# Two interleaved streams of graph batches: the distance between the streams set to 136 units in place of 111

## The chip, the core and the metric

The kernel runs on one core of one Trainium2 chip. The metric is the device time of one execution in microseconds. Five engines work side by side, each from its own queue and in the order of that queue: TensorE (PE; its weight loads are listed apart as PEld), VectorE (DVE), ScalarE (ACT), GpSimd (POOL) and SyncE (SP, which here only issues DMAs).

## What is computed

Sixteen graphs ("batches") of N = 1024 nodes with 256 features pass through four attention layers with a residual each. The batches don't depend on each other. Cut to what matters:

```python
x: (16, 1024, 256) f32        adj: (16, 1024, 1024) int32, 0 or 1, same for all layers
for layer in 0..3:
    h  = relu(layernorm(x))
    Wh = h @ W                               # layer 3: four heads of 64 columns each
    e  = act(Wh @ a1 [rows] + Wh @ a2 [columns])        # N x N scores
    p  = softmax of e (layer 1: exp(-e)) over the edges only
    y  = p @ Wh
    x  = x + y            # layers 1 and 2: x + elu(y)
    # layer 3: x + layernorm_per_head(relu(y + bias) + Wh)
```

## The kernel before, in words

All that follows is in `short_path`. (A second path, `general_path`, is entered at the end only when the inputs fall outside a tested range; here it isn't.)

**One batch.** `batch(b)` (L364) is a Python generator that issues the instructions of one batch, and ends each portion with a `yield` of a number, its nominal duration in units of about 1 us. Its portions are:

- *Projection of layer 0*, four pairs of 128-node tiles (L475 to L484). `project` (L278) has three steps of 0.5, 1.0 and 2.5 units: centre and square (L285 on DVE, L292 on ACT, and the inverse root on POOL, L271 and L272), transpose on PE (L301) and copy to `hT` on ACT (L303), then matmul (L308) into an accumulator in PSUM and evict it into `V` (L376, L380). Four pairs make 16 units.
- *Three times `attend`* (L408), for layers 0, 1 and 2. It first needs the `row` tile in PSUM. `weigh` (L317) fills it by PE (L337) and then makes eight 128x1024 weight tiles from it on DVE (L330), each of which feeds two accumulations on PE (L424, eight yields of 0.9). Then the other six 128-node outputs follow (3.6 units each), each is finished on ACT and DVE (L348 to L360, or L464), and after each second one the projection of the next layer is worked in (4 units). In sum 49.4 units.
- *Layer 3* (L493 to L654), 52.2 units. For each of four heads, `weigh3` makes eight weight tiles (L330 again; `row` by L337 or L529), PE accumulates values and totals in 32-column tiles (L541), ACT copies the sums (L618), PE turns them back (L625, L633), DVE scales them into `y` (L636), and `center` (L498) adds the bias on POOL (L502), adds the projected features `h3` on DVE (L503) and takes mean and variance (L505 to L511). `rescale` (L514) follows one head later. The output leaves by DMA (L650).

So a batch is 16 + 3 x 49.4 + 52.2 = 216.4 units, without waits.

**The two streams.** `stream(0)` issues batches 0, 2, 4, ..., 14 one after another, `stream(1)` batches 1, 3, ..., 15. Each stream has a clock that its yields advance, and a loop takes the next portion from the stream whose clock is behind:

```python
streams = [[0.0, stream(0)], [LAG, stream(1)]]
while streams:
    ahead = min(streams, key=lambda s: s[0])
    t = next(ahead[1], None)
    ...
        ahead[0] += t
```

`LAG` (L74) is where the clock of stream 1 starts. Before its first batch, each stream spends 8 units on issuing its loads (`load`, L119). The order of issue is what the framework fills the engines' queues from. It may bring an instruction forward that is ready earlier, except where `tc.keep_in_program_order` holds it.

**What the streams share.** One `row` tile (`bufs=1`, L324): a list, `row_taken`, lets only one stream use it, and the other yields 0.25 units (L322), or the rest of the `start` loop (L339), until it is given back. One `h3` and one `y` (pool `single`, `bufs=1`, L391 and L494). `h3` is written first by `evict3` (L397) in the first projection for layer 3, inside `attend(2, ...)`, and read last by L503 of head 3, at the end of layer 3. Two accumulators in PSUM for each stream (L276), two `misc` tiles in PSUM, three masks and three node tiles `x_b`, and eight weight tiles for each stream.

Of the kernel before, what the change touches and what calls it, by code (L numbers as in the profile page):

```python
# [61 lines left out]
def short_path(ctx: ExitStack, tc: tile.TileContext, ins: dict, out: bass.AP, bad: bass.AP):  # L62
# [8 lines left out]
    NH = N // HALF  # L71
    NG = HALF // P
    EXT = [3, 3, 3, 3 * H]
    LAG = 111.0  # L74
    QUAD = P // 4
    ROOT_D = D**0.5
    ROOT_E = E**0.5
# [579 lines left out]
    def stream(first: int):  # L657
        for _ in loading[first]:
            yield 2.0
        for b in range(first, B, 2):  # L660
            yield from batch(b)
# [3 lines left out]
    next(preparing)  # L665
    streams = [[0.0, stream(0)], [LAG, stream(1)]]
    while streams:
# [311 lines left out]
def tile_gat4(  # L979
# [27 lines left out]
    nc.vector.memset(ones, 1.0)  # L1007
    n_bad = flags.tile([1, 1], I32, name="n_bad")
    short_path(tc, ins, out, bad)
    with tc.tile_pool(name="flag_psum", bufs=1, space=bass.MemoryType.PSUM) as psum:  # L1010
        bads = psum.tile([1, 1], F32, name="bads")
# [39 lines left out]
```

## Time and profile before

| | |
|---|---|
| three runs | 2948.02, 2948.88, 2951.19 us (median 2948.88) |
| the profiled execution | 2950.02 us, of which the span of the trace is 2948.4 us |
| PE busy | 2810.6 us, 95% of the span |
| DVE busy | 2124.8 us, 72% |
| ACT busy | 1092.1 us, 37% |
| POOL busy | 980.7 us, 33% |
| granted TensorE clock, mean | 0.992 |

The page divides the span into 40 slices, and PE is at nine tenths or more in all of them but the first and the last two. So the questions to put to this profile are asked of short windows: where PE is idle, how often that place comes back, and what the other engines do there. A table of windows gives for each stretch the busy time of every engine with the number of instructions in brackets, and after that the granted clock, the share of the DMA engines and what they moved.

### The profile page before, as it was taken

The page shows a single profiled execution, that of the slowest core. Times are in us where ns is not written, and L with a number is a line of the kernel's source. Part 1 is how long each engine was busy: PE and PEld are TensorE (multiplying, and loading weights), DVE is VectorE, ACT ScalarE, POOL GpSimd, SP SyncE. Part 2 cuts the span into 40 slices and gives each one's busy share as a digit, 9 for nine tenths or more (in the row PEclk, how much of TensorE's full clock was granted, in tenths as well). Part 3 has the DMA queues.
Part 4 walks back from the last instruction along what each step waited for, and adds up shares of the span by engine and source line. Part 5 has one row for each costly group of instructions (what it writes and reads, how often), then busy time and mean ns, then how long its engine had stood idle before and what let it go on. Part 6 is the DMA issues. An engine that isn't in the chain of part 4 may idle for free.

```text
span 2948.4 us, 44754 instructions
## 1 busy us (share of the span) xinstructions
PE 2810.6 (95%) x16790; PEld 1969.3 (67%) x16790; DVE 2124.8 (72%) x4471; ACT 1092.1 (37%) x3025; POOL 980.7 (33%) x1535
## 2 busy tenths in 40 slices
PE   7999999999999999999999999999999999999975
PEld 5775857668576685766758576685766857667551
DVE  5658688585976858678586875859768586785855
ACT  2333434343343433424333343433434334343331
POOL 2123324243233423324233242432334233242333
PEclk9999999999999999999999999999999999999997
DMA  7204022030311303122030220303113031010101
GB/s 123 40 8 65 29 31 56 8 51 29 42 45 19 68 1 51 36 29 58 8 52 29 33 55 8 51 29 45 43 20 67 1 51 36 15 30 8 22 18 27
DMA packets 120495, 106.11 MB, mean 36 GB/s; under 512 B 73680, under 2 KB 91216, under 8 KB 120272
## 3 DMA queue, kind: packets, MB, share of 16 engines
q0 software_dynamic: 40448, 67.12, 15.4%
q1 hardware_dynamic: 79824, 36.05, 5.5%
q8 instruction: 135, 2.21, 0.3%
q14 instruction: 88, 0.72, 0.1%
HBM read 153.49 MB, written 33.55 MB: 63 GB/s over the span
## 4 chain that ended last, share of the span: by engine, by line
PE 60%; DVE 23%; issue 8%; POOL 5%; ACT 3%; DMA 1%; POOLq 0%; SPq 0%; ACTq 0%; DVEq 0%
PE acc L424 36%; DVE weights L330 16%; PE acc L541 11%; PE acc L308 9%; PE misc L301 2%; POOL rstd L272 2%; POOL y L502 2%; ACT square L292 1%; DVE V L380 1%; PE row L337 1%; DVE y L503 1%; DVE var L511 1%; DVE y L507 1%; DVE mean L505 1%; ACT below L356 1%
## 5 line engine op out<-in xcount | busy, mean ns | idle before, releaser
L424 PE MATMUL acc<-V,weights 128*128 128x257 f32 x6144 | 1436.3, 385 | 33.9 <-DVE weights L330 16.7
L424 PEld LDWEIGHTS acc<-V,weights 128*128 128x128 f32 x6144 | 1141.9, 191 | 277.9 <-DVE weights L330 72.0
L541 PE MATMUL acc<-weights,V 128*32 128x512 f32 x6144 | 692.0, 597 | 12.1 <-DVE weights L330 8.1
L330 DVE SCALAR_TENSOR_TENSOR weights<-row,ex,mask 128x1024 f32<-128x1024 f32 x512 | 629.1, 1273 | 97.4 <-PE row L529 66.0
L308 PE MATMUL acc<-W,hT 128*128 128x259 f32 (+1 forms) x2048 | 516.5, 389 | 41.7 <-ACT hT L303 29.2
L330 DVE SCALAR_TENSOR_TENSOR weights<-row,V,mask 128x1024 f32<-128x1024 f32 x384 | 473.8, 1275 | 1.0 <-PE row L337 1.0
L308 PEld LDWEIGHTS acc<-W,hT 128*128 128x128 f32 x2048 | 379.6, 191 | 138.0 <-ACT hT L303 47.1
L541 PEld LDWEIGHTS acc<-weights,V 128*32 128x32 f32 x6144 | 189.6, 110 | 417.6 <-issue 410.7
L356 ACT ACTIVATE below<-acc,inv 128x256 f32<-128x256 f32 x256 | 121.1, 473 | 818.0 <-DVE inv L349 537.3
L272 POOL TENSOR_TENSOR rstd<-rstd,minus_half 128x2 f32<-128x2 f32 (+1 forms) x320 | 302.9, 947 | 20.3
L292 ACT ACTIVATE square<-x_b,minus_mean 128x256 bf16<-128x256 f32 x512 | 259.7, 507 | 111.1 <-DVE minus_mean L282 105.4
L404 POOL TENSOR_TENSOR x_b<-x_b,beta 128x256 f32<-128x256 f32 x128 | 93.4, 730 | 489.8 <-ACT square L292 489.8
L348 DVE TENSOR_SCALAR inv<-acc 128x1 f32<-128x1 f32 x256 | 39.2, 154 | 256.0 <-PE acc L424 254.7
L271 POOL TENSOR_SCALAR rstd<-squared 128x2 f32<-128x2 f32 x256 | 64.6, 253 | 462.8 <-ACT square L292 461.9
L303 ACT ACTIVATE hT<-misc 128x512 f32<-128x512 f32 x256 | 150.1, 592 | 119.7 <-PE misc L301 119.4
L359 DVE SCALAR_TENSOR_TENSOR x_b<-below,x_b 128x256 f32<-128x256 f32 x256 | 133.0, 519 | 85.3 <-ACT below L356 83.2
L618 ACT COPY sums<-acc 128x512 f32<-128x512 f32 x128 | 74.9, 585 | 307.8 <-PE acc L541 300.3
L285 DVE TENSOR_SCALAR centered<-x_b,minus_mean 128x256 f32<-128x256 f32 x512 | 182.6, 385 | 5.3
L376 ACT ACTIVATE V<-acc,rstd 128x3 f32<-128x3 f32 x384 | 98.4, 261 | 232.0 <-PE acc L308 231.3
L380 DVE TENSOR_SCALAR V<-acc,rstd,V 128x256 f32<-128x256 f32 x256 | 131.6, 537 | 62.0 <-ACT V L376 61.1
L301 PE MATMUL misc<-ident,centered 128*128 128x128 f32 x1024 | 157.9, 277 | 15.2 <-DVE centered L285 13.4
L149 POOL DMA_DIRECT2D adj_i<-in_adj_dram x128 | 74.7, 584 | 286.4 <-ACT adj_i L154 254.9
(88 smaller groups left out, 2210.0 us busy)
## 6 DMA issues: line engine op xcount, KB each, us to landing
adj_i<-in_adj_dram POOLq DMA_DIRECT2D x128, 256.0 KB, 3.9
x_b<-in_x_dram SPq DMA_DIRECT2D x16, 1024.0 KB, 6.4
narrow<-in_adj_dram POOLq DMA_DIRECT2D x64, 256.0 KB, 9.5
out_dram<-y POOLq DMA_DIRECT2D x32, 512.0 KB, 7.4
mask<-narrow SPq DMA_TRANSPOSE x64, 3.7
W<-in_L_gnn_W_dram SPq DMA_DIRECT2D x3, 256.0 KB, 5.8
weights<-in_L_gnn_a_dram SPq DMA_DIRECT2D x3, 256.0 KB, 8.1
W<-in_L_gnn_W_dram SPq DMA_DIRECT2D x2, 128.0 KB, 8.3
```

Source lines behind the costliest of these rows:

```text
L272: nc.gpsimd.tensor_tensor(r, r, minus_half.to_broadcast([P, n]), op=ALU.pow)
L285: nc.vector.tensor_scalar(centered[:, n, :], xb[:, 2 * pair + n, :], minus_mean[:, n : n + 1], 0.0, op0=ALU.add, op1=ALU.max,)
L292: nc.scalar.activation(square, xb[:, 2 * pair + n, :], AF.Square, bias=minus_mean[:, n : n + 1], accum_out=squared[:, n : n + 1],)
L301: nc.tensor.transpose(turned[:, k, ts(n, P)], centered[:, n, ts(k, P)], ident)
L303: nc.scalar.mul(hT, turned, ROOT_D)
L308: nc.tensor.matmul(projected, hT[:, k, ts(n, P)], W[l][:, k, :], start=(k == 0), stop=(k == NK - 1),)
L330: nc.vector.scalar_tensor_tensor(w, r, c(j), masks[b][:, j // 2, :, j % 2], op0=op, op1=ALU.mult)
L356: nc.scalar.activation(below, acc[:, :D], AF.Exp, scale=inv)
L359: nc.vector.scalar_tensor_tensor(xi, below, 1.0, xi, op0=ALU.min, op1=ALU.add)
L380: nc.vector.tensor_scalar(V[:, i, :D], projected[:, :D], rstd, V[:, i, D : D + 1], op0=ALU.mult, op1=ALU.mult,)
L424: nc.tensor.matmul(accs[i], weights[j][:, ts(i, P)], V[:, j, : D + 1], start=(j == 0), stop=(j == NI - 1),)
L541: made = nc.tensor.matmul(accT[ts(n, QUAD), :], values, moving, start=first, stop=last)
```

## The change

One constant, the start of the second stream's clock, goes from 111 to 136 units:

```diff
@@ -71,7 +71,7 @@
     NH = N // HALF
     NG = HALF // P
     EXT = [3, 3, 3, 3 * H]
-    LAG = 111.0
+    LAG = 136.0
     QUAD = P // 4
     ROOT_D = D**0.5
     ROOT_E = E**0.5
```

No instruction is added or taken away. The order changes in which the portions of the two streams are issued. Of a batch of 216.4 units, 136 are 0.628, about five eighths, and 111 are 0.513.

## The prediction

> **What bounds the kernel now.** I read the page's table of engines first.
>
> ```profile
> PE 2810.6 (95%) x16790; PEld 1969.3 (67%) x16790; DVE 2124.8 (72%) x4471; ACT 1092.1 (37%) x3025; POOL 980.7 (33%) x1535
> ```
>
> PE is the bound, and is idle for 2948.4 - 2810.6 = 137.8 us. The change adds and removes no instruction, so it can only move those 137.8 us. Next, the period: SyncE's timeline shows one fetch of `x_b` at each end of a batch.
>
> ```profile
> 1023.51 0.38 SPq L115 DMA_DIRECT2D x_b<-in_x_dram  x1
> 1202.24 0.37 SPq L115 DMA_DIRECT2D x_b<-in_x_dram  x1
> ```
>
> A batch ends, in one stream or the other, every 178.73 us. Then the windows of one period:
>
> ```profile
> 1024.00:1094.00 70.00, 69.83 (x339) 59.87 (x338) 39.78 (x112) 24.39 (x75) 20.03 (x42) 1.00 0.10 31
> 1094.00:1164.00 70.00, 68.54 (x506) 35.63 (x505) 65.07 (x99) 21.97 (x52) 17.99 (x29) 1.00 0.33 39
> 1164.00:1184.00 20.00, 20.00 (x123) 14.06 (x123) 13.51 (x31) 9.79 (x23) 11.24 (x10) 1.00 0.32 54
> 1184.00:1204.00 20.00, 17.43 (x93) 14.29 (x93) 15.10 (x39) 12.12 (x40) 12.99 (x19) 1.00 0.21 28
> ```
>
> The reader should see two gaps in PE (second column). From 1094 to 1164 one stream is in layer 3, DVE is 93% busy and PE loses 1.46 us. From 1184 to 1204 a batch ends and the next one starts: PE loses 2.57 us. With 0.17 before, a period loses 4.2 us. Last the end, where stream 1 is alone:
>
> ```profile
> 2800.00:2820.00 20.00, 14.54 (x53) 10.49 (x52) 15.52 (x24) 4.06 (x12) 8.19 (x9) 0.83 0.14 52
> 2820.00:2850.00 30.00, 28.63 (x138) 23.79 (x136) 11.74 (x44) 13.56 (x42) 11.69 (x23) 1.00 0.00 1
> 2850.00:2860.00 10.00, 3.72 (x19) 2.17 (x22) 6.13 (x6) 2.24 (x8) 5.25 (x15) 0.92 0.00 0
> ```
>
> Alone, the weighing stage of an `attend` loses 5.46 us of PE, its rest 1.37 us in 30, and the step into layer 3 another 6.28 us.
>
> **What the Trainium skill says.** "Perfetto Trace Analysis", Identifying the Most-Contended Engine, warns that matmul busy time doesn't tell how near PE is to its peak. Agreed here: PE is 95% busy and its weight loads 67%; so I use idle time alone and leave PE's rate as it is. The same page, Optimization Strategy, says that a gap which comes back on the bounding engine can mean that there is no room for the next tile. The 2.57 us of before aren't that (DVE and ACT chains fill it), but the step below with `h3` would be. "TensorE: Matmul & The Clock Gate", What's actually happening, says that an idle PE falls to a lower clock until it has been busy again. The trace agrees: the granted clock is 0.83 over 2800 to 2820 and 1.00 in every steady window above. A long gap so costs more than its length.
>
> **The change, part by part.** I place everything by the nominal clock in the code. Within a batch: projection of layer 0 at 0 to 16; the three `attend` from 16, 65.4 and 114.8, the first 7.2 units of each being the weighing; layer 3 from 164.2 to 216.4.
>
> *Before*, a stream in layer 3 waits some 6 units for `row`, which the other stream's layer 1 takes between heads; a batch therefore lasts 222.3 units, and 111 is just half of it. The streams end alternately every 111.15 units, so a unit is 178.73 / 111.15 = 1.608 us. Batch start (0 to 16) lies against 111 to 127 of the other stream, the weighing of layer 2: eight L330 of 1.275 us (10.2 us of DVE) meet the projection's own DVE work and the end of layer 3. That is the 2.57 us gap.
>
> *After*, working through the yields, no stream finds `row` taken, so a batch lasts 216.4 units, and the gaps between starts alternate: 136 from an even batch to the odd one, 80.4 from the odd to the next even one.
>
> (1) *Starts of even batches, and of batch 1* (8 of the 15 starts with a partner). They now lie against 80 to 98 of the partner (batch 1: against 136), the middle of an `attend`, where PE has eight matmul groups ready and DVE no weighing. I put the remaining gap at 0.8 us, between 0.17 (the quiet 70 us above) and the 2.57 of today. Gain 8 x (2.57 - 0.8) = 14.2 us.
>
> (2) *Starts of odd batches from batch 3* (7). They lie against 136 of the partner, after the weighing of layer 2. That collision goes too, but another arrives: `h3` has one buffer. The even batch writes it first at 114.8 + 7.2 + 3.6 + 0.5 + 3.6 + 1.0 + 3.6 = 134.3 (L397). The odd batch reads it last in `center` of head 3, at 214.4 of its own, when the partner stands at 214.4 - 80.4 = 134.0. Before, the same reading stood at 220.4 - 111.2 = 109.2, so 25.1 units ahead of the write. The trace has that distance in us (lines L503 and L397 of the same pair of batches):
>
> ```profile
> L503 DVE SCALAR_TENSOR_TENSOR y<-y,h x1: 691/691/691, 1013.4 to 1013.4; 128x512 f32<-128x512 f32 x1
> L397 ACT ACTIVATE h<-acc,rstd x1: 466/466/466, 1048.8 to 1048.8; 128x256 f32<-128x256 f32 x1
> ```
>
> From the end of L503 (1014.1) to L397 are 34.7 us of room. The change takes away 25.1 - 0.3 = 24.8 units, 39.9 us. So L397 comes 5.2 us too early and has to wait. Behind it on ACT are the partner's projections; on PE, the projected tiles hold both accumulators of that stream, so its L424 stop. PE has only the new batch's projection to fill in. That is the unknown cost. Lower bound: the 10.5 us of PE work in that projection (by the page's busy times of L308 and L301 over 16 batches of 4 layers: (516.5 + 157.9) / 64) cover it and the gap falls to 0.8 as in (1). Upper bound: the whole chain from the last L541 (ending near 1003.3) to the end of L503, 10.7 us, is lost. I take the wait itself, uncovered, and the 0.8: 6.0 us, because the new batch's projection needs ACT, which is the engine that waits. Cost 7 x (6.0 - 2.57) = 24.0 us.
>
> (3) *Layer 3 against the rest* (15 times). Before, 40 L330 fall in 37 units. After, in layer 3 of an odd batch, 40 in 38 (the partner's layer 2 starts right after head 3's weighing); of an even batch, 32 in 31 and eight more at its quiet end. About as dense; I leave the 1.46 us each at that: nothing. DVE's saturation was covered by matmuls of the partner, and still is. Bounds: all 15 gaps gone, -22 us, or see the third rival.
>
> (4) *The start alone.* Stream 0 runs 25 units more by itself, through the weighing of layer 2: 5.46 us from the end's own window. Its partner before was the batch start counted in (1).
>
> (5) *The end alone.* When batch 14 is done, batch 15 stands at 80.4 instead of 111.2; 30.8 units more of quiet `attend` run alone, some 26 us at 1.37 in 30: 1.2 us. The last weighing, layer 3 and the tail are alone as before.
>
> (6) *DMAs.* SP's fetch of `x_b` is released by the end of another batch and then has 80 units, 129 us, to its use; it took 6.4 us to land. Masks likewise. Nothing, and 129 us of cover. POOL's queue carries the same instructions; in (2) its share of projection and `center` meet, which is in the upper bound.
>
> Sum: -14.2 + 24.0 + 0 + 5.5 + 1.2 = +16.5 us on the profiled 2950.0, so 2966.5; that execution was 1.1 us above the median of the runs, so I say 2965.
>
> **Rivals.** *Other side: the wait is covered.* If the planner places the new batch's projection, or more of the partner's products, under the 5.2 us, all fifteen starts fall to 0.8: -15 x 1.77 + 6.7 = -19.9, 2929 us. It decides below 3.6 us for each odd start, where 7 x (3.6 - 2.57) equals the 7.5 us that the rest of the sum gains. For it: those 10.5 us of independent work. Against: ACT is 60% busy there already and waits in order. *Nothing to measure:* the odd starts cost about what they cost now, and the ends eat the gain: 2949 - 7.5 + 7 x 1 = 2948. *Layer 3 becomes DVE-bound:* the wait for `row` used to give layer 3 six more units; without it, DVE has some 78 us of work in the odd batch's dense 38 units (40 L330, 51 us; `center` and scaling of three heads, seven operations of 0.7 us each, 14; the partner's finishing and projecting, 4.8 us in each 11.2 units of `attend`, for 31 units, 13), and 38 units last 38 x 1.608 = 61 us. Before it was 71 us (51, 14 and 6) in 37 units, 59 us. If 5 us of that reach PE in seven places, on top of my sum: 2965 + 35 = 3000 us. Against: 12 us of excess cost only 1.46 today. That the change does nothing is excluded, since the order of issue differs by 25 units throughout.
>
> **How the numbers follow.** Forecast (waits of 4 to 10 us, 2955 to 2990) 0.47; covered (2920 to 2943) 0.24; nothing to measure 0.16; DVE-bound 0.13. About 0.2% (5.9 us) is what a measurement of this kernel can tell from no change. Faster 0.24, same 0.16, slower 0.47 + 0.13 = 0.60. The range, 2930 to 2990, leaves out half of the covered case and most of the DVE-bound one, 0.2. The forecast's own range is 2955 to 2990.
>
> **What would show it.** Right: PE idle at every second batch end some 6 us, at the others under 1; the first L397 directly behind L503 of the other batch; an idle of PE or ACT ended by DVE L503; ends of batches apart by 80 and 136 units in turn, some 130 and 220 us; no more waits of layer 3 for `row`. Wrong: both kinds of ends alike, L397 tens of us after L503, or more than 2 us of idle PE in the DVE-bound stretches.

## The result and the profile after

The median is 3023.66 us of five runs (3022.9 to 3028.71), against 2949.01 before: ratio 1.0254, 95% interval 1.024 to 1.0268. That is 74.7 us slower, where 16 were forecast, and above the range. The page's first lines of the changed kernel:

```profile
span 3021.4 us, 44651 instructions
PE 2827.2 (94%) x16790; PEld 1967.5 (65%) x16790; DVE 2169.3 (72%) x4471; ACT 1095.7 (36%) x3025; POOL 974.9 (32%) x1535
```

The instructions are the same. The span is 73.0 us longer: PE is idle for 194.2 us in place of 137.8 (+56.4) and busy 16.6 us longer, at a mean granted clock of 0.984 in place of 0.992.

SyncE's timeline tells the ends of batches, by the fetch of `x_b`:

```profile
887.87 0.37 SPq L115 DMA_DIRECT2D x_b<-in_x_dram  x1
1023.60 0.38 SPq L115 DMA_DIRECT2D x_b<-in_x_dram  x1
1254.10 0.37 SPq L115 DMA_DIRECT2D x_b<-in_x_dram  x1
```

Ends follow each other after 135.7 and 230.5 us in turn, in the order that the nominal clock gave and both some 5% longer (129 and 219). A pair of batches lasts 366.2 us, where two of before last 357.5. From the first output (292.6, before 308.8) to that of batch 14 (2856.7, before 2812.45) the seven pairs cost 60.5 us more than before, and the stretches alone at both ends the other 12.5.

One pair in windows. An even batch is in the middle of layer 3 in the second line and ends in the third, at 1023.6; an odd one is in the middle of layer 3 in the fifth and ends in the sixth.

```profile
887.87:960.00 72.13, 71.83 (x457) 48.82 (x456) 56.60 (x105) 23.60 (x63) 21.70 (x42) 1.00 0.30 52
960.00:1000.00 40.00, 37.21 (x283) 18.68 (x281) 27.98 (x52) 10.22 (x25) 13.76 (x16) 1.00 0.31 54
1000.00:1030.00 30.00, 25.39 (x119) 20.17 (x120) 27.17 (x64) 16.06 (x49) 18.52 (x25) 1.00 0.30 67
1030.00:1180.00 150.00, 149.20 (x808) 116.39 (x810) 95.04 (x222) 54.24 (x158) 30.86 (x63) 1.00 0.12 16
1180.00:1215.00 35.00, 31.02 (x236) 16.03 (x240) 31.78 (x47) 13.79 (x32) 13.44 (x15) 0.95 0.31 50
1215.00:1254.10 39.10, 36.34 (x211) 25.97 (x204) 31.84 (x67) 18.64 (x52) 23.27 (x31) 0.96 0.18 24
```

First minus second number of a line is PE's idle time. Against two periods of before:

| PE idle in a pair of batches, us | before | after | forecast |
|---|---|---|---|
| layer 3, both batches | 1.46 + 1.46 | 2.79 + 3.98 | as before |
| end of the even batch | 2.57 | 4.61 | 0.8 |
| end of the odd batch | 2.57 | 2.76 | 6.0 |

So the loss went to layer 3 and to the even end, and not to the odd end, where I had put it. Of the 8.7 us that the pair is longer, 6.8 are idle PE and 1.9 are PE work that took longer.

The list of waits names the waiting instruction, then what it waited for, the total in us, the times and the longest. PE now waits for VectorE. After:

```profile
PE misc L301 <- DVE centered L285: 47.5, 26, 13.9
PE row L337 <- DVE weights L330: 18.8, 7, 2.7
```

Before, the first of these waits came to 13.4 us, and the second was not in the list:

```profile
PE misc L301 <- DVE centered L285: 13.4, 3, 12.8
```

(The longest in each, 12.8 and 13.9 us, is PE's wait for its first work at the very start.) And VectorE in turn waits for GpSimd, and ScalarE for VectorE. After:

```profile
DVE y L503 <- POOL y L502: 90.1, 49, 4.0
ACT h L397 <- DVE y L503: 7.3, 7, 1.1
```

Before, there was no such wait of L397, and of the other this much:

```profile
DVE y L503 <- POOL y L502: 27.4, 33, 2.9
```

`center` takes `y` from VectorE (L636) to GpSimd for the bias (L502) and back to VectorE (L503). The longest case after, from the timelines of VectorE and GpSimd (start and duration in us; in brackets how long the engine was idle and for whom):

```profile
963.96 0.69 DVE L636 TENSOR_TENSOR y<-misc,inv 128x512 f32<-128x512 f32 x1
964.08 0.72 POOL L272 TENSOR_TENSOR rstd<-rstd,minus_half 128x2 f32<-128x2 f32 x1
964.78 1.27 POOL L516 TENSOR_TENSOR y<-y,gamma 128x512 f32<-128x512 f32 x1
966.13 1.27 POOL L517 TENSOR_TENSOR y<-y,x_b 128x512 f32<-128x512 f32 x1
967.36 1.27 POOL L502 TENSOR_TENSOR y<-y,bias 128x512 f32<-128x512 f32 x1
968.66 0.69 DVE L503 SCALAR_TENSOR_TENSOR y<-y,h 128x512 f32<-128x512 f32 x1 [4.01 <-POOL y L502]
```

GpSimd works off three operations (L272, L516, L517) before the bias, and VectorE stands still in the middle of layer 3, with L503 at the head of its queue. The same hop, of the second head, before the change:

```profile
1155.93 0.68 DVE L636 TENSOR_TENSOR y<-misc,inv 128x512 f32<-128x512 f32 x1
...
1156.60 1.28 DVE L330 SCALAR_TENSOR_TENSOR weights<-row,ex,mask 128x1024 f32<-128x1024 f32 x1
1158.01 0.69 DVE L503 SCALAR_TENSOR_TENSOR y<-y,h 128x512 f32<-128x512 f32 x1
```

Here the queue has one L330 of 1.28 us between the two (and, where the dots stand, an L282 of 0.16 us), and it covers the hop. Not every hop before was covered by an L330. In the four heads of a batch VectorE idled 0.2, 0.1, 0 and 1.2 us in front of L503: an L330 stood between in the first two, small operations of the next projection in the other two. After the change it idles 1.4, 4.0, 1.4 and 0 us in an even batch and 2.4, 2.1, 0.2 and 0 us in an odd one, and in the five longest of these nothing at all stands between. Over the eight heads of a pair that is 11.5 us after and 3.0 before: 8.5 us more, for a pair that is 8.7 us longer. That near equality is only a hint, and the experiments have to show that the one causes the other.

How the hop reaches PE can be followed at one place, the second head of the odd batch:

```profile
1197.94 0.69 DVE L503 SCALAR_TENSOR_TENSOR y<-y,h 128x512 f32<-128x512 f32 x1 [2.13 <-POOL y L502]
1204.12 6.04 DVE L330 SCALAR_TENSOR_TENSOR weights<-row,ex,mask 128x1024 f32<-128x1024 f32 x5
1210.21 1.97 PE L337 MATMUL row<-ident,V 128*128 128x128 f32 x8 [2.68 <-DVE weights L330]
```

VectorE's queue, 2.13 us late, works off the L330 that still read `row`, and PE can fill the one `row` anew only after the last of them.

### The profile page after: what moved, and what is told of

Its sections match the earlier page's. It is cut to its first block, busy times and chain, and to the rows that moved or that the text cites. A ratio compares the mean times of both kernels' runs of the same rounds, so it can differ in the third digit from the quotient of the medians.

```text
span 3021.4 us, 44651 instructions
## 1 busy us (share of the span) xinstructions
PE 2827.2 (94%) x16790; PEld 1967.5 (65%) x16790; DVE 2169.3 (72%) x4471; ACT 1095.7 (36%) x3025; POOL 974.9 (32%) x1535
## 5 line engine op out<-in xcount | busy, mean ns | idle before, releaser
L330 DVE SCALAR_TENSOR_TENSOR weights<-row,ex,mask 128x1024 f32<-128x1024 f32 x512 | 629.9, 1275 | 47.0 <-PE row L529 42.6
L308 PE MATMUL acc<-W,hT 128*128 128x259 f32 (+1 forms) x2048 | 527.7, 395 | 46.3 <-ACT above L358 21.2
L308 PEld LDWEIGHTS acc<-W,hT 128*128 128x128 f32 x2048 | 372.5, 191 | 168.6 <-ACT above L358 43.4
L330 DVE SCALAR_TENSOR_TENSOR weights<-row,V,mask 128x1024 f32<-128x1024 f32 x384 | 471.3, 1273 | 15.2 <-PE row L337 15.2
L272 POOL TENSOR_TENSOR rstd<-rstd,minus_half 128x2 f32<-128x2 f32 (+1 forms) x320 | 300.6, 940 | 19.6
L285 DVE TENSOR_SCALAR centered<-x_b,minus_mean 128x256 f32<-128x256 f32 x512 | 197.9, 423 | 4.7
L301 PEld LDWEIGHTS misc<-ident,centered 128*128 128x128 f32 x1024 | 122.1, 142 | 104.1 <-issue 50.3
L154 ACT ACTIVATE adj_i<-adj_i,minus_half 128x1024 bf16<-128x1024 bf16 x128 | 147.3, 1151 | 14.1 <-DMA adj_i<-in_adj_dram 14.1
L509 ACT ACTIVATE wide<-y 128x512 f32<-128x512 f32 x64 | 40.3, 630 | 308.1 <-DVE y L507 291.0
```

What stands on the lines that cost most here:

```text
L154: square = nc.scalar.activation(adj_i, adj_i, AF.Square, bias=minus_half, accum_out=squares[:, b, i : i + 1])
L272: nc.gpsimd.tensor_tensor(r, r, minus_half.to_broadcast([P, n]), op=ALU.pow)
L285: nc.vector.tensor_scalar(centered[:, n, :], xb[:, 2 * pair + n, :], minus_mean[:, n : n + 1], 0.0, op0=ALU.add, op1=ALU.max,)
L301: nc.tensor.transpose(turned[:, k, ts(n, P)], centered[:, n, ts(k, P)], ident)
L308: nc.tensor.matmul(projected, hT[:, k, ts(n, P)], W[l][:, k, :], start=(k == 0), stop=(k == NK - 1),)
L330: nc.vector.scalar_tensor_tensor(w, r, c(j), masks[b][:, j // 2, :, j % 2], op0=op, op1=ALU.mult)
```

## The experiments

My theory at the start was that the loss sits at particular meeting places of 136 (`h3`, and the hand-over of `row` near 1210 us, where PE waits 2.68 us). The rival was that any unequal spacing does harm because VectorE gets too full. Times below are medians, ratios are to the kernel before in the same job.

**Other distances.** The edit is the constant alone:

```diff
-    LAG = 136.0
+    LAG = 130.0   # x1;  124.0 in x2;  142.0 in x3
```

> LAG 130: batches start 130 and 86.4 units apart in turn, still without any wait for row in the nominal clock, but layer 2 of the even batch now asks for row 6 units after head 3 of the odd batch has given it back, and first writes h3 some 10 us later than at 136. Theory 'these places' (the cost sits in the row hand-over at 1210 us and in the meeting at h3, both special to 136): at least 3 us a pair of batches back, 2995 to 3005 us. Theory 'spacing' (any spacing but the half leaves layer 3 beside the partner's finishing stages with VectorE too full): 3005 to 3025 us.

Measured: 3064.81 us, ratio 1.0384 (1.0367 to 1.0402).

> LAG 124: starts 124 and 98.4 units apart, and both batches of a pair wait for row in layer 3 again, so a batch lasts 222.4 units as at 111. Theory 'spacing': between 111 and 136, about 2975 to 3000 us. Theory 'the wait for row is what spaced layer 3 out' (the slide of 6 units is what was lost): within 10 us of before. Theory 'these places': within 15 us of before, too.

Measured: 3045.99 us, ratio 1.0321 (1.0304 to 1.0338).

> LAG 142: starts 147.8 and 74.7 units apart, even batches wait for row, odd ones' first write of h3 comes even earlier against the partner's last read (5.7 units before it). Theory 'h3': the stall of ScalarE grows by some 9 us a pair, over 3060 us. Theory 'spacing': 3030 to 3050 us. Theory 'these places' without h3: below 3023 us.

Measured: 3061.63 us, ratio 1.0379 (1.0362 to 1.0396).

All three are slower than 136. So nothing special to 136 is the cause: my theory of the places falls, and so does the one that the wait for `row` had protected layer 3, as 124 has that wait by its nominal clock and still loses 95 us. What remains is the spacing, though it costs more than its expectation said at every point. The 142 case met the number of the theory on `h3`, and shows how little such a match proves: in its trace ScalarE waits for L503 seven times, 14.8 us in all, 2.1 us each and not 9.

**Two buffers for `h3`.**

```diff
-            h3 = last["h3"] = single.tile([P, NI, D], F32, name="h3")
+            h3 = last["h3"] = single.tile([P, NI, D], BF, name="h3", bufs=2)
```

> LAG 136 with two h3 in bfloat16 in the room of one in float32 (h3 is rounded to bfloat16, the rest of the computation is kept). The forecast's step on h3: 7 stalls of 5.2 us gone, 2985 to 2990 us. What the trace of 136 shows instead (L397 directly behind L503, ScalarE idle for 1.05 us there): 3010 to 3023 us.

Measured: 3013.25 us, ratio 1.0215 (1.0198 to 1.0232). `h3` accounts for 10 of the 75 us, 1.5 us a pair of batches, and in this trace L397 no longer waits for L503. The meeting that I had worked out exists, but ScalarE loses 1.05 us at it and not 5.2.

**Less work on VectorE in layer 3.**

```diff
             if h == H:
                 return iter(())
+            if h % 2 == 1:
+                weights.extend(weights[-NI:])
+                return iter(())
```

> LAG 111, with heads 1 and 3 of layer 3 taking over the weight tiles of heads 0 and 2 (their own 256 L330 and 256 of the small row matmuls are left out, so their output is that of other weights): VectorE has 326 us less to do. PE-bound as the kernel before is, it can only win back idle PE in layer 3, at most 1.46 us x 15: 2920 to 2950 us.

Measured: 2952.76 us, ratio 1.0008 (1.0002 to 1.0015).

> The same at LAG 136 (heads 1 and 3 take over the weights of heads 0 and 2). Theory 'VectorE is too full in layer 3 beside the partner's finishing': the distance of 75 us to LAG 111 shrinks to under 30 us. Theory 'shared port of GpSimd and VectorE, or the places of h3 and row': it stays at 50 us or more.

Measured: 2972.91 us, ratio 1.0079 (1.0062 to 1.0096). At 111, some 300 us less work on VectorE (1819.4 us busy in place of 2124.8) gain nothing: there it isn't the bound. At 136 they gain 51 us, and the distance between the two shrinks from 75 to 20 us. So at 136 the time passes through VectorE's queue in layer 3. Whether through its work or its waits, this doesn't tell. (The port of the second expectation is taken up in the last section.)

**Less work on GpSimd in layer 3.** The bias addition and the multiplication by gamma are left out.

```diff
-            nc.gpsimd.tensor_add(yh, yh, bias[:, head].unsqueeze(1).to_broadcast(shape))
...
-            nc.gpsimd.tensor_mul(yh, yh, gamma[:, head].unsqueeze(1).to_broadcast(shape))
```

> LAG 111 without the bias addition and the multiplication by gamma in layer 3 (L502 and L516 left out, 166 us of GpSimd): both lie off PE's path except at the batch ends, where the chain through them is 2.6 us shorter: 2925 to 2950 us.

Measured: 2936.03 us, ratio 0.9953 (0.9936 to 0.997).

> The same at LAG 136 (bias addition and gamma left out). Theory 'small VectorE operations are held up while GpSimd works' (VectorE is 44 us busier after the change without one instruction more): the distance of 75 us to LAG 111 shrinks below 45 us. Theory 'VectorE is too full': it stays at 60 us or more.

Measured: 2907.25 us, ratio 0.9853 (0.9836 to 0.9869). The distance is not only gone, it has turned: 136 is now 29 us ahead of 111. Two operations went at once, though, and each does two things: it occupies GpSimd and it is waited for. The next runs part these.

**One operation at a time.** In x9 the bias addition (L502) alone is left out, in x10 the multiplication by gamma (L516) alone.

> LAG 136 without the bias addition alone (L502; the bias is zero in these inputs, so the output is the same). Theory 'VectorE stands in line behind L503, which waits for L502' (90 us of such waits against 27 before): most of the 117 us that both removals gave, under 2950 us. Theory 'any 1.3 us operation of GpSimd holds up small VectorE operations': about half of it, 2950 to 2975 us.

Measured: 2934.68 us, ratio 0.9944 (0.9927 to 0.9961).

> LAG 136 without the multiplication by gamma alone (L516; output unscaled by gamma). No VectorE operation waits for L516's result. Theory 'VectorE stands in line behind L503': hardly a change, 3005 to 3023 us. Theory 'any 1.3 us operation of GpSimd holds up small VectorE operations': about half of the 117 us, 2950 to 2985 us.

Measured: 2986.97 us, ratio 1.0123 (1.0106 to 1.014). L502 alone is worth 89 us, more than the whole loss. PE's two waits for VectorE fall with it:

```profile
PE misc L301 <- DVE centered L285: 18.6, 11, 14.1
PE row L337 <- DVE weights L330: 6.1, 7, 0.9
```

That is 41.6 us less of them, and PE's idle time falls by 63.8 in all (from 194.2 to 130.4). L516 is worth 37 us, which neither theory had: nobody on VectorE waits for L516, but L502 stands behind it in the timeline above, and the wait of L503 falls from 90.1 to 77.4 us without it. Where the other part of its 37 us comes from stays open.

**The bias at another place.**

```diff
+                values = V3[:, i, :, :E]
+                nc.gpsimd.tensor_add(
+                    values, h3[:, i, :].rearrange("p (h e) -> p h e", h=H),
+                    bias.rearrange("p (h e) -> p h e", h=H),
+                )
+                nc.gpsimd.tensor_mul(values, values, q.to_broadcast([P, H, E]))
-                nc.gpsimd.tensor_mul(
-                    V3[:, i, :, :E], h3[:, i, :].rearrange("p (h e) -> p h e", h=H),
-                    q.to_broadcast([P, H, E]),
-                )
...
-            nc.gpsimd.tensor_add(yh, yh, bias[:, head].unsqueeze(1).to_broadcast(shape))
```

> LAG 136, all of the computation kept: the bias is added to the values before the attention instead of after it (eight GpSimd additions of 128x256 in evict3 in place of L502's four of 128x512 a batch), since weights that are divided by their sum leave a constant as it is. GpSimd has as much to do as before, at another place. Theory 'stands in line': under 2960 us. Theory 'hold-up by GpSimd': 2975 to 3015 us, as the work meets the partner's stages elsewhere.

Measured: 2957.45 us, ratio 1.0023 (1.0013 to 1.0032).

> LAG 111 with the same fold of the bias, all of the computation kept. At the batch end the chain behind the last matmul is 1.3 us shorter, with 15 such ends: 2930 to 2945 us by both theories. If it is below the kernel before by more than 0.3%, it beats both kernels.

Measured: 2937.65 us, ratio 0.9957 (0.994 to 0.9973). GpSimd is no less busy (1002.7 us, 974.9 in the changed kernel), and still 66 of the 75 us are gone. At 111 the fold wins 13 us: with all of the computation kept, this is a version that beats both kernels. The two distances are still 20 us apart with the fold.

**Waiting or working?**

> LAG 111 without L502 (the bias is zero in these inputs). If the hop VectorE - GpSimd - VectorE is what the spacing of 136 suffers from and 111 doesn't, 111 gains little: 2935 to 2945 us, no less than the 2934.7 us of 136 without L502. If L502 costs both alike: about 2865 us.

Measured: 2937.25 us, ratio 0.9955 (0.9938 to 0.9971). L502 costs 13 us at 111 and 89 at 136. Without it the two distances are 3 us apart, 136 ahead, where they were 75 us apart with it: the loss belongs to the two together.

> LAG 130 without L502. If the 114 us that 130 costs have the same cause as the 75 us of 136: under 2970 us. If 130 has a cause of its own (its row and weight waits): over 3010 us.

Measured: 2983.58 us, ratio 1.0109 (1.0092 to 1.0126). At 130, L502 is worth 81 of the 114 us. The time lies between the two expectations, and the other 33 us are of another cause. In layer 3 PE waits there for weight tiles (L330) for 34.5 us, against 8.1 before; at 130 with L502 it was 34.8, so this wait doesn't come from the hop. I didn't follow it.

The two runs that part work from waiting put the same addition on VectorE (x15), and an equal one with no reader on GpSimd (x16):

```diff
-            nc.gpsimd.tensor_add(yh, yh, bias[:, head].unsqueeze(1).to_broadcast(shape))
+            nc.vector.tensor_add(yh, yh, bias[:, head].unsqueeze(1).to_broadcast(shape))     # x15
+            nc.gpsimd.tensor_add(spare, h3[:, :, head], bias[:, head].unsqueeze(1).to_broadcast(shape))   # x16
```

> LAG 136 with the bias addition on VectorE in place of GpSimd, all of the computation kept. VectorE gets 64 operations of 0.69 us more, 44 us, and no longer crosses to GpSimd and back. Theory 'the hop': 2935 to 2965 us, in spite of the added work on VectorE. Theory 'VectorE is too full': 3023 us or more.

Measured: 2977.76 us, ratio 1.0094 (1.0077 to 1.0111). This is 13 us above the range for the hop, and far below that of the other theory. The 44 us of added VectorE work cost 43 us against the run without L502, so here VectorE's work counts in full; and still it is 46 us better than crossing to GpSimd and back.

> LAG 136 with L502 replaced by an addition of the same size on GpSimd from h3 and the bias into a spare tile that nobody reads, so GpSimd works as long (and keeps h3 in use), but nobody waits for its result (three adj_i buffers in place of four make the room). Theory 'the hop': 2935 to 2960 us. Theory 'GpSimd's occupation and the ports it shares with VectorE': over 2990 us.

Measured: 2934.63 us, ratio 0.9949 (0.9932 to 0.9966). This is the time without L502, to 0.1 us, although GpSimd works no less than in the changed kernel:

```profile
span 2933.5 us, 44678 instructions
PE 2803.2 (96%) x16790; PEld 1954.8 (67%) x16790; DVE 2156.3 (74%) x4471; ACT 1090.4 (37%) x3025; POOL 992.8 (34%) x1535
```

So the loss is the crossing and not GpSimd's work. (The spare tile takes the room of one of four `adj_i` buffers, which I did not try alone; x9, which has all four, takes the same time.) VectorE's timeline of that run, at the place of the 4.01 us above (a line added to the kernel moves L636 to L637 and L503 to L504):

```profile
943.17 0.69 DVE L637 TENSOR_TENSOR y<-misc,inv 128x512 f32<-128x512 f32 x1
943.90 0.69 DVE L504 SCALAR_TENSOR_TENSOR y<-y,h 128x512 f32<-128x512 f32 x1
```

The two follow each other at once. The crossing has a second half, which no run parts from the first: L502 waits on GpSimd for L636, and holds up what stands behind it there, and the dummy doesn't wait for L636 either. That GpSimd's half is what the change made worse is unlikely, since its idle time in front of L502 fell, from 191.9 us to 143.1.

**The order on GpSimd.** A try to shorten the hop and keep it: issue `center` ahead of `rescale`, so that L502 doesn't stand behind L516 and L517.

```diff
-            if h > 0:
-                rescale(*normed.pop())
             normed.append(center(h))
+            if h > 0:
+                rescale(*normed.pop(0))
```

> LAG 136 with center of a head issued ahead of rescale of the head before it, all of the computation kept: L502 no longer stands behind L516 and L517 on GpSimd (at 964 us of the trace after, the bias addition begins 2.71 us late for that, and VectorE is idle for 4.01 us). Theory 'VectorE waits for L502 in layer 3': the late part goes, the 1.3 us of L502 itself stays; idle of VectorE before L503 falls from 90 us to 40 to 60, and the time to 2960 to 3000 us. If the wait only shows where VectorE has nothing to do: 3015 to 3030 us.

Measured: 3023.73 us, ratio 1.0248 (1.0231 to 1.0266).

> LAG 111 with the same swap, all of the computation kept. L502 began within 0.1 us of L636's end in three of four heads, so there is little to gain: 2940 to 2952 us by both theories; above that if rescale's later start holds up the output.

Measured: 2950.38 us, ratio 0.9999 (0.999 to 1.0008). GpSimd's timeline of x17 at the place of the 4.01 us:

```profile
964.53 1.27 POOL L516 TENSOR_TENSOR y<-y,gamma 128x512 f32<-128x512 f32 x1
965.88 1.27 POOL L517 TENSOR_TENSOR y<-y,x_b 128x512 f32<-128x512 f32 x1
967.10 1.27 POOL L502 TENSOR_TENSOR y<-y,bias 128x512 f32<-128x512 f32 x1
```

The queue has the old order at this place: the planner (the part of the framework that fills the queues) took L516 and L517 first all the same, presumably since they were ready first. So the run didn't do what it was made for, and is inconclusive. That L516 and L517 make the wait longer is read from the timeline, and backed by x10, but not shown by an order that differs in nothing else.

## Why the prediction was wrong, step by step

**The direction** was right, and by luck: the one cost that was to give it, step (2), is the smaller part of the loss. **(2)**, the meeting of `h3`, was placed correctly and sized wrong: L397 comes directly behind L503 at every odd end, as forecast, but ScalarE waits 1.05 us, and the odd end lost 2.76 us of PE against 2.57, where 6.0 were forecast. The room of 34.7 us was measured in the queue of before; where the other 4 us of the wait went, no run shows. By x4, `h3` costs 10 us in all, the forecast's step 24.

**(1)**, the relief of the even ends, failed. Forecast was a fall from 2.57 to 0.8 us, and the even end loses 4.61. Without L502 it still loses 2.55 (978 to 1008 us in x9), much as before the change, so that the relief is missing even without the hop.

**(3)** is the step whose mechanism failed: "About as dense; I leave the 1.46 us each at that: nothing. DVE's saturation was covered by matmuls of the partner, and still is." There I counted L330 for a stretch, 40 in 37 units before and 40 in 38 after. What I didn't count was the order in VectorE's queue. Before, other work stands between L636 and L503 in every head of a steady batch, and covers most of the hop to GpSimd. After, in five of eight heads nothing stands there, and VectorE idles 8.5 us more in a pair, at times when its later work is due. The two layers 3 lose 6.77 us of PE in place of 2.92. My own sign of being wrong, more than 2 us of idle PE in such a stretch, came true in both (2.79 and 3.98). The third rival named layer 3 as VectorE-bound, and gave 3000 us for it with a chance of 0.13; x6 and x15 show that it had the right engine. But it reasoned from the amount of work, which the change leaves as it is, and what the change adds is the wait: L502 gone (x9), moved (x11), or kept with no reader (x16) gives back 89, 66 and 89 us.

**(4) and (5)**, the ends: 6.7 us forecast, 12.5 measured. **(6)**, the DMAs, cost nothing, as forecast. **The clock** wasn't in the sum: PE is busy 16.6 us longer, at a lower mean clock. That an idle PE falls to half its clock is what the Trainium skill says ("TensorE: Matmul & The Clock Gate", What's actually happening), after an idle window of about 3.4 us. The trace agrees in kind, but a shorter gap was enough: with the single gap of 2.68 us that ends at 1210.21, the granted clock is 0.50 from 1209.56 to 1212.97, which gives the window 1180 to 1215 its 0.95. The even end, with 4.61 us in gaps of at most 1.92, stays at 1.00. In x16, which has fewer gaps, the mean clock is 0.993 again.

In sum, the forecast for the pairs was -14.2 + 24.0, some 10 us, and measured are 60.5. If all seven pairs are like the one in windows (an estimate from its lines), layer 3 cost 27 us where nothing was forecast, the even ends 14 where a gain of 14.2 was, the odd ends 1 where 24.0 was, the other stretches 5, and the clock 13. The ends of the run cost the other 12.5. Why unequal spacing leaves VectorE's queue without work at the hop, and the half spacing does not, is a matter of the planner's order, which I only read from the timelines. That the larger losses at other distances are mainly the same hop is shown for 130 alone; VectorE's waits of L503 are 59.9 us there, 65.4 at 124 and 64.0 at 142, less than the 90.1 at 136, so their sum alone doesn't rank the losses.

## What to carry to other kernels

Here, two interleaved streams hid each other's waits only where the order in the queues put other work between the two halves of a hop; so when their distance is changed, go through the hops from one engine to another and back, and see for each what is queued between, rather than compare sums of work by stage. A hop out of a dense in-order queue and back can cost far more than the operation on the other side: the same 64 additions cost 13 us at one distance and 89 at another. It paid to remove the hop (here, by adding the bias to the values before the attention): 66 us at 136 and 13 at 111. The distance still matters after that: 20 us between 136 and 111 with the fold, and 46 between 130 and 111 without L502.

## What the runs showed of the hardware that was not expected

A small operation of VectorE can last as long as an operation of GpSimd that runs at the same time. VectorE's and GpSimd's timelines of the changed kernel at an even end:

```profile
1020.98 1.25 POOL L516 TENSOR_TENSOR y<-y,gamma 128x512 f32<-128x512 f32 x1
1021.06 1.32 DVE L285 TENSOR_SCALAR centered<-x_b,minus_mean 128x256 f32<-128x256 f32 x1
1022.31 1.26 POOL L517 TENSOR_TENSOR y<-y,x_b 128x512 f32<-128x512 f32 x1
1022.37 1.34 DVE L285 TENSOR_SCALAR centered<-x_b,minus_mean 128x256 f32<-128x256 f32 x1
```

L285 has a median of 0.35 us, and here takes 1.32 and 1.34, each ending just after GpSimd's operation. "SBUF — State Buffer", Who interferes with whom, in the Trainium skill, has this: the two engines share a pair of ports, and the one that comes second is blocked for the whole instruction of the other. It says so for certain operations of VectorE, and its tensor_scalar, which L285 is, can be one of them. These two lines agree. VectorE's busy time grew by 44.5 us without one instruction more (2124.8 to 2169.3); the mean of L285 rose from 385 to 423 ns, which over 512 of them makes 19.5 us of it. It was the natural suspect, and x16 clears it of most of the loss: VectorE is at 2156.3 us there, so that 13.0 of the 44.5 us are gone, and the time is 89 us shorter.
